# Edges read as 80 short rows and a written order for the first stage in a graph layer kernel

## The chip, the cores and the metric

The kernel runs on one core of a Trainium2 chip. The metric is the device time of one execution in microseconds (us), taken as the median of several runs. All profiles are of one execution on that core.

## What is computed

The reference is one layer of a graph transformer over 625 nodes of width 1024 with 20,000 edges. The first norm feeds a two-layer graph convolution and a linear attention, whose outputs are added to x; then a mixture of eight experts is added. Cut to what matters here:

```
xn = layernorm(x)
deg = segment_sum(ones, dst);  deg_inv = 1 / max(deg, 1)
sage(h, Ws, Wn, b) = h @ Ws + (segment_sum(h[src], dst) * deg_inv) @ Wn + b
gnn = sage(relu(sage(xn, Ws0, Wn0, b0)), Ws1, Wn1, b1)
q, k, v = xn @ Wq, xn @ Wk, xn @ Wv
mix = softmax(q over features) * 1/8 @ (softmax(k over nodes)^T @ v) @ Wo + bo
x = x + gnn + mix
x = x + moe(layernorm(x))
```

The edges come sorted by dst. The sum over edges is done as a product with a 625 x 625 matrix of edge counts, which the kernel counts from src and dst.

## The kernel before, in words

All float32 products are made of three matmuls on rounded parts. A tensor is split into a high part (a cast on ScalarE) and a low part (a subtraction on VectorE or GpSimd); `split` at L96 does both, so every such pair has line L96. `xnh` and `xnl` are the two parts of the transposed first norm, `whi` and `wlo` those of a weight tile. A weight tile is 512 KB, is loaded by SyncE's queue into `wraw` (three buffers, L121) and is split when `Stream.next` (L127) hands it out. Its argument says which engine does the low part; without one it is VectorE.

**The first stage.** The 625 rows of x are five tiles of 128 rows (the last has 113). SyncE's queue issues tiles 0 and 1, the edge lists, one key weight tile, then tiles 2 to 4 (L305 to L311). The edge lists `src` and `dst` are read as 10 rows of 2000 numbers each into `ei` (L308). Each x tile gets its statistics (`first_stats`, L250 and L251), its scale (`inv_std`, L254 to L260, a chain of tiny VectorE operations with one square root on ScalarE), is normalised in place (`first_norm`, even tiles on VectorE L330, odd ones on ScalarE L328) and is transposed on TensorE and split into `xnh` and `xnl` (`first_turn` to `to_t`, L278 and L96). Tiles 0 and 1 share one scale chain, tiles 2 to 4 another.

**The edges.** `edges` is the float copy of `ei` (L336), over 10 partitions. 32 small transposes (L340) and one more for the first dst of each row (L345) put 125 edges on 125 partitions: a chunk is 125 edges, a group is 16 chunks, and there are 10 groups, 160 chunks in all. GpSimd derives `field`, `srow` and `unit` (L438 to L446) and makes `edst` relative to the first dst of its group.

**The counting.** For each chunk VectorE writes a pair of one-hot matrices, 125 x 128 each (`one_hot`, L456 and L457), into a ring `hot` of 40 places. TensorE multiplies each pair (L479) and sums the 16 chunks of a group in `pa`; VectorE adds that to `packed` at a column that it reads from a register (L481, L483). A pair is written only when its place in the ring has been multiplied.

**The key steps.** `keys_step` makes K and the self product of the first convolution: 16 weight tiles, four steps each, 64 steps. A step is 12 matmuls (L400 to L402). The first three weight tiles take the columns of x tiles 0 and 1 first (256 columns, steps 0 to 5), then the other 370 columns (steps 6 to 11); the rest take 314 and 312. After a key tile is complete `keys_exp` takes its maximum over nodes on VectorE (L378), negates it (L379) and exponentiates on ScalarE (L380); a few steps later `keys_back` transposes it on TensorE into `pskt` (L372). In the main loop (L499 to L502) each step is followed by four one-hot pairs and the product of four chunks; 36 pairs are made ahead of it (L495).

**What sets the order.** Each engine has one queue, in strict order. A scheduler places instructions by priority; `tc.high_priority()` raises a block, `keep` (keep_in_program_order) fixes the order of the marked instructions on their engine, and `issue_after` holds something behind a named instruction. Before, only the loads, the statistics' first operation, some transposes and GpSimd's edge chain are marked.

## Time and profile before

| what | us |
|---|---|
| median of three runs | 1042.17 |
| lowest, highest run | 1039.62, 1044.56 |
| the profiled execution | 1041.26 |
| its span | 1039.7 |
| TensorE busy in it | 1010.3 |
| VectorE, ScalarE, GpSimd busy | 601.3, 396.2, 175.6 |
| first key matmul starts | 25.13 |
| one-hots written | 36.61 to about 129 |
| chunk products | 56.2 to 143.8 |

PE is TensorE's matmul, PEld its weight load, DVE VectorE, ACT ScalarE, POOL GpSimd and SP SyncE. A line of the page's second part has 40 digits, each the busy share in tenths of one fortieth of the span, here 26 us. A line of the timeline has the start, the length, the engine, the line of code, the operation, the tiles written and read, their sizes, and in brackets how long the engine had been idle and what ended that. A line of the waits names who waited for whom, the total, how often, and the longest. The times come from one profiled execution, and the text compares its sum with that execution's own time.

### The profile page before, as it was taken

The numbers are of one execution on the slowest core, as the hardware profiler recorded it, in microseconds if no ns is written. First come the engines' busy times: TensorE is split into PE (matmuls) and PEld (weight loads), VectorE is DVE, ScalarE is ACT, GpSimd is POOL, SyncE is SP. The second block draws the span as 40 slices with busy tenths as digits, with TensorE's granted clock in tenths as the row PEclk, the third lists the DMA queues.
The fourth block names the chain that finished last, engine by engine and source line by source line (L and its number), as shares of the span: only waits on it lengthen the run. The fifth ranks groups of instructions, "written<-read, shape, count | busy, mean of one in ns | idle before, by whom it ended". The sixth has DMA issues, their size and how long they took to land. (4 is left out here: it accounts for less than half of the span.)

```text
span 1039.7 us, 14793 instructions
## 1 busy us (share of the span) xinstructions
PE 1010.3 (97%) x5571; PEld 871.6 (84%) x5571; DVE 601.3 (58%) x1192; ACT 396.2 (38%) x577; POOL 175.6 (17%) x222
## 2 busy tenths in 40 slices
PE   6889999999999999999999999999999989999998
PEld 4889998888888887988877899998879777887786
DVE  3899941653253233733327536358687688887681
ACT  3333432232231122222114332246556567766610
POOL 2421001121035300200000103022121033120030
PEclk7999999999999999999999999999999999999999
DMA  6122225665234421232220125666967798897971
GB/s 186 56 67 59 64 77 187 234 205 198 79 111 151 160 82 64 67 115 78 82 81 21 42 63 189 191 184 189 284 235 229 243 304 293 288 290 247 329 260 51
DMA packets 111312, 164.68 MB, mean 158 GB/s; under 512 B 5919, under 2 KB 63271, under 8 KB 111230
## 3 DMA queue, kind: packets, MB, share of 16 engines
q1 hardware_dynamic: 97774, 118.54, 35.9%
q0 software_dynamic: 13456, 45.08, 12.9%
q8 instruction: 47, 0.77, 0.3%
q14 instruction: 35, 0.29, 0.1%
HBM read 133.19 MB, written 30.42 MB: 157 GB/s over the span
## 5 line engine op out<-in xcount | busy, mean ns | idle before, releaser
L96 DVE TENSOR_TENSOR wlo<-wraw,whi 128x1024 fp32r<-128x1024 f32 x140 | 178.1, 1272 | 263.1 <-ACT whi L96 262.0
L96 ACT CAST whi<-wraw 128x1024 fp32r<-128x1024 f32 x149 | 156.4, 1051 | 290.0 <-PE psg L207 66.2
L1137 PE MATMUL pse<-xs,whi 128*128 128x448 f32 (+1 forms) x384 | 109.1, 357 | 0.0
L96 DVE TENSOR_TENSOR wlo<-wmore,whi 128x1024 fp32r<-128x1024 f32 x67 | 87.0, 1299 | 26.8 <-ACT whi L96 25.7
L1133 PE MATMUL pse<-xs,wlo 128*128 128x224 f32 (+1 forms) x384 | 89.7, 254 | 0.1
L96 ACT CAST whi<-wmore 128x1024 fp32r<-128x1024 f32 x67 | 70.5, 1052 | 47.7 <-PE psz L207 18.5
L400 PE MATMUL psk<-xnh,whi 128*128 128x314 f32 (+3 forms) x256 | 82.9, 325 | 0.4 <-ACT xnh L96 0.4
L401 PE MATMUL psk<-xnl,whi 128*128 128x314 f32 (+3 forms) x256 | 79.6, 311 | 0.9 <-DVE xnl L96 0.8
L402 PE MATMUL psk<-xnh,wlo 128*128 128x314 f32 (+3 forms) x256 | 79.5, 311 | 0.2 <-POOL wlo L96 0.2
L1189 PE MATMUL psy<-wlo,he 128*128 128x512 f32 (+1 forms) x176 | 70.0, 398 | 3.3 <-DVE wlo L96 3.0
L1133 PEld LDWEIGHTS pse<-xs,wlo 128*128 128x128 f32 x384 | 72.0, 190 | 1.4 <-DVE wlo L96 0.3
L1137 PEld LDWEIGHTS pse<-xs,whi 128*128 128x128 f32 x384 | 69.0, 189 | 2.4
L1188 PE MATMUL psy<-whi,he 128*128 128x512 f32 (+1 forms) x176 | 69.4, 394 | 0.0
L1190 PE MATMUL psy<-whi,he 128*128 128x512 f32 (+1 forms) x176 | 69.0, 392 | 0.0
L457 DVE TENSOR_SCALAR hot<-iota,srow,unit 125x128 f16<-125x128 f16 x160 | 59.7, 373 | 0.0
L96 POOL TENSOR_TENSOR xs<-raw,xs 128x512 fp32r<-128x512 f32 (+2 forms) x24 | 34.4, 1454 | 115.6 <-ACT xs L96 95.0
L401 PEld LDWEIGHTS psk<-xnl,whi 128*128 128x128 f32 x256 | 49.5, 193 | 1.3 <-DVE xnl L96 1.3
L400 PEld LDWEIGHTS psk<-xnh,whi 128*128 128x128 f32 x256 | 49.2, 193 | 0.8 <-ACT xnh L96 0.8
L402 PEld LDWEIGHTS psk<-xnh,wlo 128*128 128x128 f32 x256 | 49.1, 192 | 0.4 <-POOL wlo L96 0.4
L456 DVE TENSOR_SCALAR hot<-iota,edt 125x128 f16<-125x128 f16 x160 | 45.8, 286 | 1.7 <-POOL edt L446 1.7
L1189 PEld LDWEIGHTS psy<-wlo,he 128*128 128x128 f32 (+1 forms) x176 | 31.8, 180 | 14.9 <-DVE wlo L96 6.7
L1188 PEld LDWEIGHTS psy<-whi,he 128*128 128x128 f32 (+1 forms) x176 | 31.9, 181 | 10.1
(348 smaller groups left out, 2379.5 us busy)
## 6 DMA issues: line engine op xcount, KB each, us to landing
wraw<-in_L_ffn_w_dram SPq DMA_DIRECT2D x65, 512.0 KB, 4.8
wmore<-in_L_ffn_w_dram SPq DMA_DIRECT2D x63, 512.0 KB, 5.4
xsd<-zt POOLq DMA_DIRECT2D x9, 1024.0 KB, 5.6
wraw<-in_L_gnn_W_self_dram SPq DMA_DIRECT2D x16, 512.0 KB, 3.7
wraw<-in_L_gnn_W_neigh_dram SPq DMA_DIRECT2D x16, 512.0 KB, 3.7
wraw<-_ffn_shared_gate_up_dram SPq DMA_DIRECT2D x16, 512.0 KB, 3.9
wraw<-in_L_mix_Wk_dram SPq DMA_DIRECT2D x8, 512.0 KB, 4.1
wraw<-in_L_mix_Wq_dram SPq DMA_DIRECT2D x8, 512.0 KB, 3.7
```

The costliest lines, as they stand in the source:

```text
L96: return (nc.scalar.copy(hi, srcap), (eng or nc.vector).tensor_sub(lo, srcap, hi.bitcast(F32)))
L400: nc.tensor.matmul(ps[:, :n], wh[:, kt, :], xnh[:, kt, c], start=kt == 0, stop=False)
L401: nc.tensor.matmul(ps[:, :n], wh[:, kt, :], xnl[:, kt, c], start=False, stop=False)
L402: nc.tensor.matmul(ps[:, :n], wl[:, kt, :], xnh[:, kt, c], start=False, stop=kt == KT - 1)
L456: nc.vector.tensor_scalar(h[:ET, :WIN], iota[:ET, :WIN], edst[:, i, g:g + 1], None, op0=ALU.is_equal)
L457: nc.vector.tensor_scalar(h[:ET, WIN:], iota[:ET, :WIN], srow[:ET, i, g:g + 1], unit[:ET, i, g:g + 1].bitcast(F32), op0=ALU.is_equal, op1= ...
L1133: nc.tensor.matmul(ps[a][:, :n], wl[:, k, c], xs[:, kt, 0, :], start=False, stop=False)
L1137: nc.tensor.matmul(ps[a][:, :2 * n], wh[:, k, c], xs[:, kt], start=kt == 0, stop=kt == KT - 1)
L1188: nc.tensor.matmul(acc, h(kt, 0), wh[:, k, :], start=kt == 0, stop=False)
L1189: nc.tensor.matmul(acc, h(kt, 0), wl[:, k, :], start=False, stop=False)
L1190: nc.tensor.matmul(acc, h(kt, 1), wh[:, k, :], start=False, stop=kt == KT - 1)
```

## The change

It has five parts.

1. The edge lists are read as 80 rows of 250 numbers (`EP` = 80), issued on ScalarE's queue, into small tiles of their own. Four transposes of 80 x 125 replace the 32, and `edt`, `field`, `srow` and `unit` get a new layout, [half, group, row in group]; which edges form a chunk changes within a group, not what a group holds. The big buffers no longer hold `ei` and `edges`.
2. SyncE's queue issues a key weight tile ahead of each of x tiles 2, 3 and 4.
3. Each x tile has a scale chain of its own (`first_scale`), and all are normalised on ScalarE.
4. The whole first stage is written out in one order, and nearly all its VectorE, ScalarE and GpSimd instructions are kept in it: two key steps, turn of tile 2, two steps, turn of tile 3, two steps, turn of tile 4. The edge transposes stand behind the turns of tiles 0 and 1.
5. In the counting, 40 pairs are made ahead; then three a step up to step 40 and four after it, made behind the products and no longer ahead of them. The register read for `packed` is held behind the last pair made so far. Key weight tiles 3 to 8 get their low part on VectorE, no longer on GpSimd.

The core of the diff:

```diff
+EP = E // (2 * ET)
...
-    ei = big.tile([128, 2, CH * ET], I32, name="ei", tag="big")
+    ei = edgep.tile([EP, 2, 2 * ET], I32, name="ei")
...
-    for t in range(2):
-        load_x(t)
+    load_x(0)
+    load_x(1)
     for i, e in enumerate((src, dst)):
-        keep(nc.sync.dma_start(ei[:NG, i, :], e.rearrange("(p c) -> p c", p=NG)))
-    st.load(1)
+        keep(nc.scalar.dma_start(ei[:, i, :], e.rearrange("(p c) -> p c", p=EP)))
     for t in range(2, NT):
+        st.load(t - 1)
         load_x(t)
...
+    def first_scale(t):
+        inv_std(lnv[:T, t:t + 1, 1], *(lnt[:T, i, t:t + 1] for i in range(3)), order=keep)
+        keep(nc.vector.scalar_tensor_tensor(lnt[:T, 1, t:t + 1], lnv[:T, t:t + 1, 0], -1.0, lnt[:T, 0, t:t + 1],
+                                            op0=ALU.mult, op1=ALU.mult))
+
+    def first_norm(t):
+        p = rows(t)
+        keep(nc.scalar.activation(xts[p, t, :], xts[p, t, :], AF.Identity,
+                                  bias=lnt[p, 1, t:t + 1], scale=lnt[p, 0, t:t + 1]))
...
+    def turn_edges():
+        pse = bank("psed")[:, :4 * EP].rearrange("p (a b) -> p a b", b=EP)
+        for i in range(4):
+            nc.tensor.transpose(pse[:ET, i, :], edges[:, i // 2, (i % 2) * ET:(i % 2 + 1) * ET], ident[:EP, :EP])
+        keep(nc.scalar.copy(edt[:ET].rearrange("p a h g j -> p (a h) (g j)"), pse[:ET]))
...
-        if s in (0, 2, 4):
-            wks[o] = st.next(nc.gpsimd)
         if (o, i, h) == (1, 1, 0):
-            wks[3] = st.next(nc.gpsimd)
+            wks[3] = st.next()
         if i == 0 and h == 0 and 2 < o < 2 * KT - 1:
-            wks[o + 1] = st.next(nc.gpsimd if o < KT else None)
+            wks[o + 1] = st.next()
...
+    def keys_weights(o):
+        wks[o] = st.next(nc.gpsimd, order=keep)
...
     with tc.high_priority():
-        keys_steps(4)
+        first_stats(0)
+        first_scale(0)
+        first_norm(0)
+        keep(nc.scalar.copy(edges, ei))
+        first_stats(1)
+        first_scale(1)
+        keys_weights(0)
+        first_norm(1)
+        first_stats(2)
+        first_turn(0)
+        first_turn(1)
+        turn_edges()
+        keys_weights(1)
+        first_scale(2)
+        first_norm(2)
         first_stats(3)
+        first_scale(3)
+        keys_weights(2)
+        first_norm(3)
+        keys_steps(2)
+        first_turn(2)
         first_stats(4)
-        first_norm(2, NT)
-        first_turn(2, keep)
+        first_scale(4)
+        first_norm(4)
         keys_steps(2)
-        first_turn(3, keep)
-        last = first_turn(4, keep)
+        first_turn(3)
+        keys_steps(2)
+        last = first_turn(4)
...
+                with tc.issue_after(hots[-1].ins):
+                    first_v = nc.vector.value_load(first_col[0:1, g:g + 1], min_val=0, max_val=N - 1)
...
-        one_hots(RING - 4)
+        one_hots(RING)
...
     while ks[0] < 8 * KT:
         keys_steps(1)
-        one_hots(4)
         count_chunks(4)
+        one_hots(3 if ks[0] < 5 * KT else 4)
```

The gathers of 128 rows are the indirect reads of the experts' outputs near the end; the change leaves them as they are.

More of the change, by code (lines that the diff above doesn't have):

```diff
@@ L93, in bank, with split @@
         return psum.tile([128, 512], F32, name=name, tag="ps")
-    def split(srcap, hi, lo, eng=None):
-        return (nc.scalar.copy(hi, srcap), (eng or nc.vector).tensor_sub(lo, srcap, hi.bitcast(F32)))
+    def split(srcap, hi, lo, eng=None, order=lambda ins: ins):
+        return (order(nc.scalar.copy(hi, srcap)), order((eng or nc.vector).tensor_sub(lo, srcap, hi.bitcast(F32))))
     class Stream:
@@ L125, in load, with next @@
                 self.loaded += 1
-        def next(self, eng=None):
+        def next(self, eng=None, **order):
             if self.ready:
@@ L139, in next @@
                 lo = wts.tile([128, D], F32R, name="wlo", tag="wlo")
-            split(r, hi, lo, eng)
+            split(r, hi, lo, eng, **order)
             b = ap.shape[2]
@@ L250, in stats, with inv_std @@
                 order(nc.vector.bn_stats(st6[:mv.shape[0], h, :], xt[:, h * 512:(h + 1) * 512]))
-        nc.vector.bn_aggr(mv, st6[:mv.shape[0]])
-    def inv_std(var, y, z, a):
-        nc.vector.tensor_scalar(a, var, EPS, None, op0=ALU.add)
-        nc.scalar.activation(y, a, AF.Sqrt)
-        nc.vector.reciprocal(y, y)
-        nc.vector.tensor_mul(z, y, y)
-        nc.vector.tensor_mul(z, z, a)
-        nc.vector.tensor_scalar(z, z, -0.5, 1.5, op0=ALU.mult, op1=ALU.add)
-        nc.vector.tensor_mul(y, y, z)
+        (order or (lambda ins: ins))(nc.vector.bn_aggr(mv, st6[:mv.shape[0]]))
+    def inv_std(var, y, z, a, order=lambda ins: ins):
+        order(nc.vector.tensor_scalar(a, var, EPS, None, op0=ALU.add))
+        order(nc.scalar.activation(y, a, AF.Sqrt))
+        order(nc.vector.reciprocal(y, y))
+        order(nc.vector.tensor_mul(z, y, y))
+        order(nc.vector.tensor_mul(z, z, a))
+        order(nc.vector.tensor_scalar(z, z, -0.5, 1.5, op0=ALU.mult, op1=ALU.add))
+        order(nc.vector.tensor_mul(y, y, z))
     def normalise(eng, yt, xt, mean, y, z):
@@ L271, in by_k, with to_t @@
         return nat.rearrange("p (c k) -> p k c", k=KT)
-    def to_t(nat, t, hi, lo, order=None):
+    def to_t(nat, t, hi, lo, order=None, both={}):
         for g in range(2):
@@ L280, in to_t @@
                     order(tr)
-            done = split(ps[:, :, rows(t)], hi[:, 4 * g:4 * g + 4, cols(t)], lo[:, 4 * g:4 * g + 4, cols(t)])
+            done = split(ps[:, :, rows(t)], hi[:, 4 * g:4 * g + 4, cols(t)], lo[:, 4 * g:4 * g + 4, cols(t)],
+                         **both)
         return done
@@ L318, in first_stats @@
         stats(xts[rows(t), t, :], lnv[rows(t), t, :], order=keep)
-    def first_norm(a, b):
-        inv_std(lnv[:T, a:b, 1], lnt[:T, 0, a:b], lnt[:T, 1, a:b], lnt[:T, 2, a:b])
-        y, z = lnt[:T, 0, :], lnt[:T, 1, :]
-        nc.vector.scalar_tensor_tensor(z[:, a:b], lnv[:T, a:b, 0], -1.0, y[:, a:b], op0=ALU.mult, op1=ALU.mult)
-        for t in range(a, b):
-            p = rows(t)
-            xt = xts[p, t, :]
-            if t % 2:
-                nc.scalar.activation(xt, xt, AF.Identity, bias=z[p, t:t + 1], scale=y[p, t:t + 1])
-            else:
-                nc.vector.tensor_scalar(xt, xt, lnv[p, t, 0:1], y[p, t:t + 1], op0=ALU.subtract, op1=ALU.mult)
@@ L332, in first_turn @@
-    def first_turn(t, order=None):
-        return to_t(xts[rows(t), t, :].rearrange("p (k c) -> p k c", c=128), t, xnh, xnl, order)
-    edges = big.tile([128, 2, CH * ET], F32, name="edges", tag="big")
-    nc.scalar.copy(edges[:NG], ei[:NG])
-    edt = edgep.tile([128, 2 * CH, NG], F32, name="edt")
-    pse = bank("psed")[:, :2 * CH * NG].rearrange("p (a b) -> p a b", b=NG)
-    for i in range(2 * CH):
-        nc.tensor.transpose(pse[:ET, i, :], edges[:NG, i // CH, (i % CH) * ET:(i % CH + 1) * ET], ident[:NG, :NG])
@@ L341, in gps_layer @@
-    nc.scalar.copy(edt[:ET], pse[:ET])
-    esrc, edst = edt[:ET, :CH, :], edt[:ET, CH:, :]
-    psf = bank("psf")
-    nc.tensor.transpose(psf[:, :NG], edges[:NG, 1, 0:1].to_broadcast([NG, 128]), ident[:NG, :NG])
+    def first_scale(t):
+        inv_std(lnv[:T, t:t + 1, 1], *(lnt[:T, i, t:t + 1] for i in range(3)), order=keep)
+        keep(nc.vector.scalar_tensor_tensor(lnt[:T, 1, t:t + 1], lnv[:T, t:t + 1, 0], -1.0, lnt[:T, 0, t:t + 1],
+                                            op0=ALU.mult, op1=ALU.mult))
@@ new lines, in first_norm, with first_turn @@
+    def first_norm(t):
+        p = rows(t)
+        keep(nc.scalar.activation(xts[p, t, :], xts[p, t, :], AF.Identity,
+                                  bias=lnt[p, 1, t:t + 1], scale=lnt[p, 0, t:t + 1]))
+    def first_turn(t):
+        return to_t(xts[rows(t), t, :].rearrange("p (k c) -> p k c", c=128), t, xnh, xnl, keep, dict(order=keep))
+    edges = edgep.tile([EP, 2, 2 * ET], F32, name="edges")
+    edt = edgep.tile([128, 2, 2, NG, CH // 2], F32, name="edt")
+    esrc, edst = edt[:ET, 0], edt[:ET, 1]
@@ L346, in gps_layer @@
     first_dst = edgep.tile([128, NG], F32, name="first_dst")
-    nc.scalar.copy(first_dst, psf[:, :NG])
     first_col = edgep.tile([1, NG], I32, name="first_col")
-    with tc.high_priority():
-        for t in range(2):
-            first_stats(t)
-        first_norm(0, 2)
-        first_stats(2)
-        for t in range(2):
-            first_turn(t)
+    def turn_edges():
[3 more added lines that the diff above has]
+        keep(nc.scalar.copy(edt[:ET].rearrange("p a h g j -> p (a h) (g j)"), pse[:ET]))
+        psf = bank("psf")
+        nc.tensor.transpose(psf[:, :EP], edges[:, 1, 0:1].to_broadcast([EP, 128]), ident[:EP, :EP])
+        keep(nc.scalar.copy(first_dst, psf[:, :EP].rearrange("p (g j) -> p g j", g=NG)[:, :, 0]))
@@ L422, in keys_steps @@
                 keys_step(k)
+    def keys_weights(o):
+        wks[o] = st.next(nc.gpsimd, order=keep)
     with tc.high_priority():
-        keys_steps(4)
-        first_stats(3)
+        first_stats(0)
[13 more added lines that the diff above has]
+        first_norm(2)
+        first_stats(3)
+        first_scale(3)
[3 more added lines that the diff above has]
+        first_turn(2)
         first_stats(4)
-        first_norm(2, NT)
-        first_turn(2, keep)
+        first_scale(4)
+        first_norm(4)
         keys_steps(2)
-        first_turn(3, keep)
-        last = first_turn(4, keep)
-    field = edgep.tile([128, CH, NG], F32, name="field")
-    srow = edgep.tile([128, CH, NG], F32, name="srow")
-    unit = edgep.tile([128, CH, NG], I32, name="unit")
+        first_turn(3)
+        keys_steps(2)
+        last = first_turn(4)
+    field = edgep.tile([128, 2, NG, CH // 2], F32, name="field")
+    srow = edgep.tile([128, 2, NG, CH // 2], F32, name="srow")
+    unit = edgep.tile([128, 2, NG, CH // 2], I32, name="unit")
     keep(nc.gpsimd.tensor_scalar(field[:ET], esrc, 1.0 / T, -0.496, op0=ALU.mult, op1=ALU.add))
@@ L445, in gps_layer @@
                                  op0=ALU.mult, op1=ALU.add))
-    keep(nc.gpsimd.tensor_sub(edst, edst, first_dst[:ET, None, :].to_broadcast([ET, CH, NG])))
+    keep(nc.gpsimd.tensor_sub(edst, edst, first_dst[:ET, None, :, None].to_broadcast([ET, 2, NG, CH // 2])))
     keep(nc.gpsimd.tensor_copy(first_col, first_dst[:1]))
@@ L455, in one_hot @@
     def one_hot(h, i, g):
-        nc.vector.tensor_scalar(h[:ET, :WIN], iota[:ET, :WIN], edst[:, i, g:g + 1], None, op0=ALU.is_equal)
-        nc.vector.tensor_scalar(h[:ET, WIN:], iota[:ET, :WIN], srow[:ET, i, g:g + 1],
-                                unit[:ET, i, g:g + 1].bitcast(F32), op0=ALU.is_equal, op1=ALU.mult)
-    pa, made, counted = [None], [0], [0]
+        e = (slice(0, ET), i // 8, g, slice(i % 8, i % 8 + 1))
+        nc.vector.tensor_scalar(h[:ET, :WIN], iota[:ET, :WIN], edst[e], None, op0=ALU.is_equal)
+        return nc.vector.tensor_scalar(h[:ET, WIN:], iota[:ET, :WIN], srow[e], unit[e].bitcast(F32),
+                                       op0=ALU.is_equal, op1=ALU.mult)
+    pa, made, counted, hots = [None], [0], [0], []
     def one_hots(n):
@@ L466, in one_hots @@
                 made[0] += 1
-                one_hot(hot[:, c % RING, :], c % CH, c // CH)
+                hots.append(one_hot(hot[:, c % RING, :], c % CH, c // CH))
     def count_chunks(n):
@@ L480, in count_chunks @@
             if i == CH - 1:
-                first_v = nc.vector.value_load(first_col[0:1, g:g + 1], min_val=0, max_val=N - 1)
+                with tc.issue_after(hots[-1].ins):
+                    first_v = nc.vector.value_load(first_col[0:1, g:g + 1], min_val=0, max_val=N - 1)
                 to = packed[:T, ds(first_v, WIN)]
@@ L559, in recount @@
         ct = tmp.tile([128, HW], F32, name="ct", tag="tmp")
-        nc.vector.tensor_tensor(edst, edst, first_dst[:ET, None, :].to_broadcast([ET, CH, NG]), op=ALU.add)
+        nc.vector.tensor_tensor(edst, edst, first_dst[:ET, None, :, None].to_broadcast([ET, 2, NG, CH // 2]), op=ALU.add)
         nc.vector.tensor_scalar(field[:ET], esrc, float(HW), None, op0=ALU.is_ge)
@@ L569, in recount @@
                     h = tmp.tile([128, WIN + HW + 1], F16, name="hrare", tag="tmp")
-                    nc.vector.tensor_scalar(h[:ET, :WIN], iota[:ET, :WIN], edst[:, i, ds(g, 1)], None, op0=ALU.is_equal)
-                    nc.vector.tensor_scalar(h[:ET, WIN:WIN + HW], iota[:ET, :HW], esrc[:, i, ds(g, 1)],
-                                            field[:ET, i, ds(g, 1)], op0=ALU.is_equal, op1=ALU.mult)
+                    nc.vector.tensor_scalar(h[:ET, :WIN], iota[:ET, :WIN], edst[:, i // 8, ds(g, 1), i % 8], None, op0=ALU.is_equal)
+                    nc.vector.tensor_scalar(h[:ET, WIN:WIN + HW], iota[:ET, :HW], esrc[:, i // 8, ds(g, 1), i % 8],
+                                            field[:ET, i // 8, ds(g, 1), i % 8], op0=ALU.is_equal, op1=ALU.mult)
                     nc.tensor.matmul(ps[:, :HW], h[:ET, :WIN], h[:ET, WIN:WIN + HW], start=i == 0, stop=i == CH - 1)
```

## The prediction

> **What bounds the kernel now.** I read the page first, then the waits of TensorE, then the timeline of the first 75 us engine by engine.

> From the page: busy time, the slices and the clock.

> ```profile
> span 1039.7 us, 14793 instructions
> PE 1010.3 (97%) x5571; PEld 871.6 (84%) x5571; DVE 601.3 (58%) x1192; ACT 396.2 (38%) x577; POOL 175.6 (17%) x222
> ...
> PE   6889999999999999999999999999999989999998
> ...
> PEclk7999999999999999999999999999999999999999
> ```

> TensorE bounds nearly everything; its low slices are the first three. The waits of PE (total us, times, longest) name its idle time:

> ```profile
> PE psed L340 <- ACT edges L336: 6.8, 1, 6.8
> PE pskt L372 <- ACT shared L380: 3.0, 1, 3.0
> PE psy L1189 <- DVE wlo L96: 3.0, 4, 1.5
> PE pst L278 <- DVE xts L330: 2.0, 1, 2.0
> ```

> No PE wait from 175 us on ends with a weight transfer, so a PE that starts earlier should end earlier. The timeline (start, length) gives the stage that the change rewrites:

> ```profile
> 11.09 3.51 ACT L336 CAST edges<-ei 10x4000 f32<-10x4000 int32 x1
> ...
> 14.74 6.86 PE L340 MATMUL psed<-ident,edges 10*125 10x10 f32 x32 [6.75 <-ACT edges L336]
> ...
> 42.05 0.43 PE L401 MATMUL psk<-xnl,whi 128*128 128x370 f32 x1 [0.80 <-DVE xnl L96]
> 65.64 0.77 PE L372 MATMUL pskt<-ident,shared 128*128 128x128 f32 x5 [2.96 <-ACT shared L380]
> ```

> A cast over ten rows, then 32 tiny transposes, stand in PE's queue ahead of the first x transposes, normalised since 11.2. From 42.05 PE streams 370 columns every 0.17 us; it stops once more, 62.68 to 65.64. That stop begins on VectorE, which reaches the maximum for the exp late, having lost time three times like this (DVE, then POOL):

> ```profile
> 47.23 2.50 DVE L457 TENSOR_SCALAR hot<-iota,srow,unit 125x128 f16<-125x128 f16 x1
> 47.27 2.40 POOL L96 TENSOR_TENSOR wlo<-wraw,whi 128x1024 fp32r<-128x1024 f32 x1 [10.57 <-ACT whi L96]
> ```

> A one-hot of 0.31 us lasts as long as POOL's instruction beside it; again at 54.42 (2.41), 56.75 (2.43) and, later, at 67.01, 79.71 and 87.22. The stop is paid twice (windows: span, busy PE, PEld, DVE, ACT, POOL, clock):

> ```profile
> 67.00:68.00 1.00, 1.00 (x6) 1.00 (x6) 1.00 (x2) 0.16 (x1) 1.00 (x1) 0.54 0.00 0
> 68.00:69.00 1.00, 1.00 (x7) 0.81 (x6) 1.00 (x1) 0.00 (x0) 1.00 (x1) 0.50 0.00 0
> ```

> Matmuls stand 0.26 apart instead of 0.145 from 67.1 to 70.4: 3.3 us at half rate, 1.6 lost.

> **Part 1: the first stage, up to key step 6 (PE at 42.05).** PE's order after that point is unchanged, so I carry the new queues forward to it, with before's durations.

> Arrivals: x0 is used at 4.53. Ahead of x2 now stand x0, x1 and Wk0; x2 was used at 11.18 and has the 20 edge rows of 8 KB no longer before it on its queue, so I take 10.9 at latest. The 7 us slice moved 73 GB/s where its neighbours move 295 and 166: that was the edge rows. Now they are 160 rows of 1000 bytes, issued on ACT after its table load: two issues of 0.41 and 0.30 (their SP rows) from 2.5, where ACT idles. They should land by 8; no row shows it, so from 5 (x0 landed 3.6 after its issue) to 12 (the slowest landing of the stage, 10 after issue). Up to 9 is free; each us later is a us in ACT's queue (sqrt 1, whi 0, norm 1 stand behind the cast).

> Scale and norm: statistics and aggregate 1.53 (4.53 to 6.06); from there to the scaled mean 1.62. DVE: tile 0 ready 7.7, tile 1 10.9. The norms of tiles 0, 2 and 4 move from DVE (0.81) to ACT (1.24), which I count there. ACT: norm 0 (1.24) to 8.95, cast of 500 elements a row (3.51 x 500/4000, with overhead 0.5) to 9.5, sqrt 1, whi 0 (1.05) to 10.75, norm 1 to 12.15. PE: turn 0 at 9.0, turn 1 at 12.2.

> [...] Before, the clock fell to half at 12.5, after PE idled from 8.0, and rose at 26.1, 4.5 us after the x transposes began at 21.6. [...] 12.5, 26.1, 67.1, 70.4 lie whole multiples of 3.41 apart; a window 42% busy fell, one 60% busy did not. [...] with half clock from 12.5 to 15.9 turn 1 lasts to 14.0, the five edge transposes (0.2 each) to 15.1. By before's row of half clock to 26.1, stage 1 would lose 4 more. [...]

> Then: xnh (0.59 each) to 14.6; edge copies 0.43 and 0.17 to 15.6; whi 1 to 16.65. Steps 0-1, 24 matmuls of 0.12, from 15.1, partly at half clock, to 18.4. POOL's wlo 1 runs 16.7 to 19.05 and the scale of tile 2 meets it: before, L254 took 2.21 instead of 0.17 beside such an instruction. So scale 2 ends at 19.5 (18.1 without that). Norm 2 to 20.75, turn 2 20.8 to 21.9, steps 2-3 to 24.8 (wlo 1 in time). ACT: psk copy 0.37, sqrt 3, whi 2 to 22.5, xnh, norm 3 to 24.3, xnh to 24.85; wlo 2 at 24.95. Turn 3 to 25.9, steps 4-5 to 28.8. DVE: two xnl to 25.55, statistics 4 to 27.05, scale 4 to about 29 beside POOL's small operations; norm 4 to 30.2, turn 4 from there, xnh at 31.3, xnl at 31.95. PE is at the point of 42.05 at 31.95: **10.1 sooner**. ACT carries about 18 of those 24 us and sets the pace; PE waits 1.4 for norm 4. Bounds: 12 if no lock or half clock bites, 6 if half clock stays to 26 and some ten handovers cost 0.2 more. Nearest to the rows used: 10.

> **Part 2: the keys and the counting.** Removed: six POOL splits (2.4 each), each stopping a one-hot for some 2.15: 13 us. What POOL then does before its fill at 162 is nothing, so no one is let through earlier there. Added: the same splits on DVE, 1.27 each (the row of L96 DVE): 7.6. Queued behind each on DVE are the one-hots; waiting for it are PE's next key tile and, in the new order, the negated maximum. 40 pairs are made ahead instead of 36, then 3 a step.

> From the issue order of the changed program: 11.5 pairs, wlo 3, max 0, 28.5 pairs, max 1, wlo 4, mx 1. A pair costs 0.385 (twelve from 42.45 to 47.06). Pairs start at 32.55; POOL's field chain, 4.9 from 24.95, is done at 30. wlo 3 ends at 38.35 (its whi waits for step 7, 36.0), max 0 at 39.1, exp 0 with its table load 41.6; PE asks at 44.15, so no wait. 28 pairs to 50.3, max 51.0, wlo 4 52.25, exp 1 53.35. PE asks 20.63 after step 6 as before (62.68 - 42.05), at 52.6: a wait of **0.8** replaces 2.96, too short for the clock. The transposes of 65.64 come at 53.4, 12.2 sooner, and the 1.6 of half clock goes: **13.8**.

> After that a group of four steps takes PE 8.75 and DVE 12 x 0.385 + 0.72 + 1.27 + 0.15 + 0.29 = 7.05: PE stays the bound, cover 1.7. At four pairs a step it is 16 x 0.385 + 1.6 = 7.8, still under. Counting ends at the same step; register loads stand directly ahead of an add now too (90.40, no gap), so nothing. The DMA issues moved ahead on SP are of the same count; x4 now waits for x0 to land (4.5), needed at 25: nothing. The edge tiles leave the six big buffers, and the same six are then held by the same tiles: nothing. Bounds of part 2 beyond part 1: 1.5 (DVE two us later: 2.8 waited, half clock again) to 4.5 (no wait).

> **Sum.** Profiled execution 1041.3 (span 1039.7) - 13.8 = 1027.5. It lies 0.9 under the median 1042.2, so 1028.

> **Rivals.**
> Half clock stays and ACT's handovers pile up: gain 6 + 2 to 4, say 9, so **1033**. For: ACT is one chain of some 30 instructions, each waiting on another engine. Against: PE's sustained work starts at 12.2 rather than 21.6.
> Cleaner start: no lock, windows fall well: 12 + 4.5, **1025**.
> No gain: the weight stream is the true pace from 800 us on, where DMA is 0.89 busy, and takes the gain back: **1042**. For: that share. Against: no PE wait there names a transfer.
> Slower: DVE becomes the bound of the counting. If splits between the pairs break their overlap, a pair costs its two page means, 286 + 373 ns = 0.66. By 0.275 a pair: 28 pairs delay exp 1 by 7.7; six groups cost 12 x 0.275 - 1.7 = 1.6 each, 9.6; the last two and a half, 16 x 0.275 - 1 = 3.4 each, 8.5. 25.8 - 13.8 = 12 slower, **1054**. It decides from a pair of about 0.57. Against: 0.385 is the spacing wherever POOL is still.
> That the change does not do what it says is ruled out by the issue order.

> **Chances.** Likeliest 0.68 (own range 1024 to 1032), half clock 0.18, cleaner 0.06, no gain 0.05, slower 0.03. The range 1022 to 1035 takes the first three with the spread of the runs (1039.6 to 1044.6). A change under 0.5% can't be told from none here; faster by more means under 1037: 0.92, same 0.05, slower 0.03.

> **What would show it.** Right: the first key matmul at 14 to 16 (25.13 before), the 370-column stream at 30 to 34, the second pskt at 52 to 56 with a wait under 1.4, clock 1.0 there, no one-hot over 0.5 us until 140. Wrong: edges landing after 12; half clock beyond 19; DVE waits on the new splits; PE waits on pa or wlo after 60; or a wait on wraw late in the kernel.

## The result and the profile after

The changed kernel took 1031.96 us (median of 4 runs, 1029.49 to 1032.83) beside 1042.51 for the kernel before on the same chip (4 runs). The ratio is 0.9897, with a 95% interval of 0.9867 to 0.9927. Run once more, unchanged, it took 1029.82 (6 runs) beside 1039.9, a ratio of 0.9891 (0.9867 to 0.9915). So it is about 1% faster, and the gain is 10 to 11 us where 13.8 was forecast. The profiled execution of the changed kernel took 1032.83 with a span of 1031.2, 8.5 under the span before.

The page after (the head, busy times, TensorE's slices and its clock):

```profile
span 1031.2 us, 14763 instructions
PE 1004.8 (97%) x5543; PEld 866.2 (84%) x5543; DVE 595.3 (58%) x1216; ACT 397.7 (39%) x583; POOL 160.2 (16%) x216
...
PE   7999999999999999999999999999999999999798
...
PEclk8999999999999999999999999999999999999899
```

The first slices are better, as intended. But at the right end, slice 38 of both lines, there is a new dip of TensorE and of its clock, which the kernel before does not have there. The count has changed too: 28 matmuls fewer (5571 before), and as many weight loads. Both facts turn out to be the same story.

TensorE's waits after name the new idle time:

```profile
PE pst L279 <- ACT xts L329: 5.8, 4, 1.9
PE psz L206 <- issue: 5.2, 1, 5.2
```

The wait of 6.8 for the cast of the edges is gone, and the 3.0 before the second `pskt` is down to 0.6. Four handovers from ScalarE in the first stage cost 5.8. The second line is new in size: 5.2 us in which nothing that the profile records holds TensorE back. It is just behind a branch.

The early part went nearly as worked out (timeline of the changed kernel: start, length, and in brackets idle time and releaser). These are the cast of the edges, their transposes, the matmul that answers to 42.05 before, and the second `pskt`, at 65.64 before:

```profile
9.12 0.59 ACT L424 CAST edges<-ei 80x500 f32<-80x500 int32 x1
14.06 0.97 PE L345 MATMUL psed<-ident,edges 80*125 80x80 f32 x4
31.87 0.44 PE L393 MATMUL psk<-xnl,whi 128*128 128x370 f32 x1
53.05 0.77 PE L366 MATMUL pskt<-ident,shared 128*128 128x128 f32 x5 [0.56 <-ACT shared L374]
```

The last chunk is multiplied at 129.7 (143.8 before) and the last matmul of the experts' second product, `psy`, starts 14.2 sooner, at 964.6 where it was 978.8. Then come a branch at L1255 (L1237 before) around a loop for experts with more rows than their places, which is jumped over here, and the last product of all, the shared expert's `psz`. Here is that place in the kernel before, from the timeline:

```profile
978.80 0.39 PE L1190 MATMUL psy<-whi,he 128*128 128x512 f32 x1
980.63 0.47 PE L205 MATMUL psz<-whi,sth 128*128 128x512 f32 x1 [1.45 <-DVEq L1237]
```

And in the changed kernel:

```profile
964.57 0.39 PE L1208 MATMUL psy<-whi,he 128*128 128x512 f32 x1
970.12 0.77 PE L206 MATMUL psz<-whi,sth 128*128 128x512 f32 x1 [5.16 <-issue]
```

The wait rose from 1.45 to 5.16. The windows behind it (length, then busy time and count of PE, PEld, DVE, ACT, POOL; then the clock, the share of the DMA engines, GB/s) show a second price:

```profile
968.00:969.00 1.00, 0.00 (x0) 0.00 (x0) 0.00 (x0) 0.00 (x0) 0.00 (x0) 0.50 0.72 223
971.00:972.00 1.00, 1.00 (x4) 0.71 (x4) 0.00 (x0) 0.00 (x0) 0.54 (x1) 0.50 1.01 377
```

The clock was at half from 967.8 to 974.6. In that stretch the matmuls stand 0.43 us apart, behind it 0.23. The count in brackets takes in every matmul that reaches into the window, so it is no count of starts. From the first `psz` to the end it takes 61.08 (1031.2 - 970.12), before 59.07 (1039.7 - 980.63). So 3.7 of wait and 2.0 of slower matmuls give back 5.7 of the 14.2, and 8.5 is left, which is the difference of the spans.

```profile
q8 instruction: 1, 0.02, 6.0%
```

```profile
q8 instruction: 1, 0.02, 6.3%
```

By its times in the trace, the packet before ran from 973.65 to 974.61, so it began about 5.5 ahead of the end of the products at 979.2; none ran in the wait itself. After, there is none from 960 on until one that ran from 967.62 to 968.63, 2.7 us into the wait that began at 964.96; the first `psz` follows its end by 1.5. The edges lost 28 transposes with their weight loads, 56 TensorE instructions, so everything behind them moved up by 56 places in the stream. The place at which the next block is fetched, if it is tied to the count, did not move. 28 matmuls at the 0.227 of their spacing here are 6.4 us: by this estimate the fetch that came about 5.5 ahead of the jump should come about 1 behind it; it is seen 2.7 behind it. By the code the jump is over some 230 instructions. At which count a packet is asked for, no run here shows. The rival was that the transfers around that jump, which keep the DMA engines busy (share 0.72 and 1.01 in the two windows above), happened to hold something up in this run.

### The profile page after: what moved, and what is told of

Its sections match the earlier page's. It is cut to its first block, busy times and chain, and to the rows that moved or that the text cites. A ratio compares the mean times of both kernels' runs of the same rounds, so it can differ in the third digit from the quotient of the medians.

```text
span 1031.2 us, 14763 instructions
## 1 busy us (share of the span) xinstructions
PE 1004.8 (97%) x5543; PEld 866.2 (84%) x5543; DVE 595.3 (58%) x1216; ACT 397.7 (39%) x583; POOL 160.2 (16%) x216
## 5 line engine op out<-in xcount | busy, mean ns | idle before, releaser
L97 DVE TENSOR_TENSOR wlo<-wraw,whi 128x1024 fp32r<-128x1024 f32 x146 | 185.0, 1267 | 266.3 <-ACT whi L97 262.0
L97 ACT CAST whi<-wmore 128x1024 fp32r<-128x1024 f32 x67 | 70.4, 1051 | 53.4 <-PE psz L208 24.3
L474 DVE TENSOR_SCALAR hot<-iota,srow,unit 125x128 f16<-125x128 f16 x160 | 49.8, 311 | 0.0
L1206 PEld LDWEIGHTS psy<-whi,he 128*128 128x128 f32 (+1 forms) x176 | 31.9, 181 | 10.1
L473 DVE TENSOR_SCALAR hot<-iota,edt 125x128 f16<-125x128 f16 x160 | 40.1, 251 | 0.2 <-issue 0.2
```

What stands on the lines that cost most here:

```text
L97: return (order(nc.scalar.copy(hi, srcap)), order((eng or nc.vector).tensor_sub(lo, srcap, hi.bitcast(F32))))
L473: nc.vector.tensor_scalar(h[:ET, :WIN], iota[:ET, :WIN], edst[e], None, op0=ALU.is_equal)
L474: return nc.vector.tensor_scalar(h[:ET, WIN:], iota[:ET, :WIN], srow[e], unit[e].bitcast(F32), op0=ALU.is_equal, op1=ALU.mult)
L1206: nc.tensor.matmul(acc, h(kt, 0), wh[:, k, :], start=kt == 0, stop=False)
```

## The experiments

Twelve kernels were run, in four groups. Each group shares the runs of the kernel before, whose median was 1039.9 in the first (16 runs), 1040.4 in the second (30), 1042.0 in the third (10) and 1040.8 in the fourth (11). "Key step 6" is here the matmul that answers to 42.05 of before, and "last chunk" the last chunk's product, at 143.8 before.

### The wait at the jump

**Unchanged** (again):

> The changed kernel once more, nothing edited. Theory A (the loss at the end is a fetch of a 16 KB block of TensorE's instructions, set by how many instructions stand before the jump over the overflow experts): the wait ahead of the first psz is again 5 to 5.3 us and the time again 10 to 11 us under the kernel before. Theory B (the fetch met other traffic in that one execution): the wait is 1 to 3 us this time, and the profiled time some 4 us lower.

1029.82. The wait was 4.06, again put down to `issue`, with half clock behind it. That is less than the 5 to 5.3 of theory A and more than the 1 to 3 of theory B. Key step 6 came at 31.08 and the last chunk at 128.9. A chance in one run it is not.

**More warm-up matmuls** (page28):

```diff
-WARM = 20
+WARM = 48
-        nc.tensor.matmul(psw, cold[:, :128], cold, start=i == 0, stop=i == WARM - 1)
+        nc.tensor.matmul(psw[:, :213], cold[:, :128], cold[:, :213], start=i == 0, stop=i == WARM - 1)
```

> The changed kernel with its 20 warm-up matmuls of 512 columns cut into 48 of 213: the same array time, and 28 pairs of weight load and matmul more, which is what the edge transposes lost, so that every later TensorE instruction has the place it had before the change. Theory A: the wait ahead of the first psz is 1.4 us as before the change, no half clock after it, and the time is 5 to 6 us under the unedited changed kernel, about 1026. Theory B: the wait is what it was, and the time within 1.5 us of the unedited changed kernel.

1026.15 (ratio 0.9853, 0.9828 to 0.9877), 3.7 under the unchanged one, where 5 to 6 was expected. The wait is 1.45 and no half clock follows. The gain on the kernel before is now 13.75. In its profile key step 6 was later, at 33.03: of its two windows of half clock in the first stage one fell on 22.4 to 25.8, where in the unchanged run both lie together, 13.6 to 20.4. But the warm-up is different too, so by itself this run did not prove the case.

**Fewer of them** (pagem8), `WARM = 12`, 16 instructions less than the changed kernel:

> The changed kernel with 12 warm-up matmuls instead of 20, so 16 TensorE instructions fewer. [...] Theory A: no fetch ahead of the first psz (1 to 2 us), but the next block is asked for late too, so up to 3 us may be lost some 30 instructions on; time 2 to 6 us under the unedited changed kernel, less what a colder clock in the first 10 us costs (under 1.5). Theory B: the same 5 us wait or a random one.

1029.4 (0.9892, 0.9866 to 0.9917), the changed kernel's own time; the profile is of the slowest of its six runs, 1034.91. The wait did not vanish and did not stay; it moved (timeline):

```profile
969.79 0.47 PE L206 MATMUL psz<-whi,sth 128*128 128x512 f32 x1 [1.45 <-DVEq L1255]
970.10 0.40 PE L207 MATMUL psz<-wlo,sth 128*128 128x512 f32 x1
973.05 0.80 PE L208 MATMUL psz<-whi,stl 128*128 128x512 f32 x1 [2.55 <-issue]
```

TensorE passes the jump, does a few matmuls and then stands, in the middle of a run of products, and the view names no releaser. The packet of the fetch ran from 970.85 to 971.84, inside this stop.

**Instructions that never run** (unexecuted). 28 further matmuls are put inside an earlier branch, the one for rare edges at L776, whose body is jumped over:

```diff
-                    nc.tensor.matmul(ps[:, :n], g0h[rows(s), s, o * 128:(o + 1) * 128], al[rows(s), c0:c0 + n],
-                                     start=True, stop=True)
+                    for _ in range(29 if (s, o, c0) == (0, 0, 0) else 1):
+                        nc.tensor.matmul(ps[:, :n], g0h[rows(s), s, o * 128:(o + 1) * 128], al[rows(s), c0:c0 + n],
+                                         start=True, stop=True)
```

> The changed kernel with 28 further matmuls and weight loads inside the branch for rare edges, whose body is jumped over and never executed: everything that runs is the changed kernel's, in its order, and only the place of TensorE's later instructions in its stream moves, by 56, to where it was in the kernel before. If the place of the branch over the overflow experts decides: the wait there is 1.45 to 2.2 instead of 4.1 to 5.2 and no half clock follows, and the time falls by 3 to 5 from 1029.8, to 1025 to 1027, with the first stage as it was (key step 6 at 30 to 31). Rival: the version with 28 more warm-up pairs gained its 3.7 in the first stage, by other warm-up matmuls; then the wait or the time stays, at 1029 to 1031.

1024.55 (1023.25 to 1026.47; ratio 0.984, 0.9815 to 0.9864), 5.3 under the changed kernel by code that nothing executes. The wait (timeline):

```profile
964.32 0.47 PE L206 MATMUL psz<-whi,sth 128*128 128x512 f32 x1 [1.49 <-DVEq L1256]
```

The page has 47 packets of q8 again, and the packet of the fetch is ahead again, as this line of the DMA view of 956 to 957 shows:

```profile
q8 instruction: 1, 0.02, 8.8%
```

From the first `psz` to the end it took 59.08 (1023.4 - 964.32), as before. The wait is 2.57 shorter than in the unchanged run and the rest 2.69 (61.77 there): together 5.3, the difference of the medians. TensorE came to the jump at 962.8 in both profiles. The rival of this run, that the first stage made the gain, falls: key step 6 was even later, at 33.14. (A window of half clock at 187.6 to 191.1 in the unchanged run, which this one lacks, made most of that up.)

**The kernel before, moved** (beforemoved): the same edit in the kernel before, with 100 matmuls (`range(101 ...)`). This number, like the 16 instructions of pagem8, comes from my estimate of where a block begins; no run here shows that place itself.

> The kernel before with 100 further matmuls and weight loads inside the same branch, never executed: 200 instructions[...]. If the place decides: the wait before the first psz rises from 1.45 to 4 or 5 and half clock follows it, and the time rises by 3 to 5.7, to 1043 to 1046 beside 1040.4. Rival: what matters is something else of the changed kernel (its transfers, the time at which it arrives); then the wait stays 1.45 and the time 1040 to 1041. The longer jump over the enlarged body may itself cost up to 2 by its wait before the first psag, which was 1.5.

1050.9 (1047.14 to 1052.1; ratio 1.0086, 1.0063 to 1.011), 10 slower, more than expected. Two waits of TensorE did it (the waits view; 1.4 and 1.5 in the kernel before):

```profile
PE psz L205 <- PEq L1238: 4.6, 1, 4.6
PE psag L785 <- DVE wlo L96: 4.0, 1, 4.0
```

The first is the one that was meant: 3.2 longer, with half clock from 986.3 to 993.1, and 61.45 from the first `psz` on instead of 59.07, in all 5.6. The second is the jump over the body that I had enlarged by 200 instructions. It waits 2.5 longer, with half clock from 412.8 to 419.6; I had allowed 2 for it. The releaser that the view names there is not what it waited for: a packet of the fetch ran from 410.69 to 412.11 in that wait, and the matmuls start at 413.51. So the place in the stream is shown to be the cause from both sides, in both kernels, without touching anything that runs.

**The fetch in all profiles.** That the link is the fetch is read from the packets of all fourteen profiles. In seven (before, page28, unexecuted, edgespage, oldedges, pagescale, scalefour) TensorE waits 1.45 to 2.16 at the jump, and the packet begins 5.0 to 6.4 us before TensorE gets there. In six (the profile after, again, beforemoved, edgesonly, lowpool, oldcount) it waits 3.23 to 5.16, and the packet begins 0.5 to 2.7 us after TensorE got there. In pagem8 the packet is in the later stop. In all these long stops, with the second one of beforemoved eight, the next matmul starts 1.2 to 1.8 us after the packet's end.

### Which part gives the 14

**The edges alone** (edgesonly): the kernel before with 80 rows on ScalarE's queue, four transposes and the new layout.

```diff
-        keep(nc.sync.dma_start(ei[:NG, i, :], e.rearrange("(p c) -> p c", p=NG)))
+        keep(nc.scalar.dma_start(ei[:, i, :], e.rearrange("(p c) -> p c", p=EP)))
...
-    for i in range(2 * CH):
-        nc.tensor.transpose(pse[:ET, i, :], edges[:NG, i // CH, (i % CH) * ET:(i % CH + 1) * ET], ident[:NG, :NG])
+    for i in range(4):
+        nc.tensor.transpose(pse[:ET, i, :], edges[:, i // 2, (i % 2) * ET:(i % 2 + 1) * ET], ident[:EP, :EP])
```

> The kernel before with the edges part alone: 80 rows on ACT's queue, four transposes, the tiles by halves. TensorE's instruction count is that of the changed kernel. If the edges are the main part of the early gain: key step 6 about 6 to 8 sooner than before (34 to 36 instead of 42.05), the stop before the second pskt about 3 as before, since GpSimd's low parts stay, the last product of the counting some 6 to 8 sooner; and by the instruction-block theory a wait of 4 to 5 at the jump and a half clock after it, which gives some 5.7 of that back: 1038 to 1040 in all. Rival: the written order, not the edges, makes the early gain; then key step 6 is at 40 or later and the time is 1042 or more, above before by the block's loss. Rival of the block theory: the wait at the jump stays 1.45, and the time is 1033 to 1035.

1039.03, ratio 0.9985 (0.9968 to 1.0002): no difference that can be told, over 20 runs from 1033.0 to 1044.6. Yet in its profile key step 6 is at 34.83 (7.2 sooner) and the last chunk at 134.4 (9.4 sooner). The wait at the jump is 4.1 and the end takes 60.4. So the largest part of the change, made alone, gives almost nothing. The profiled run is one of the shortest of the 20, 1033.84, so it does not show all of why.

**The edges alone, put back in place** (edgespage), with the 28 warm-up pairs of page28:

> The edges alone, as in the run of 1039.0, with the 28 further warm-up pairs that put the branch back to where it stood in the kernel before. If the block of instructions takes the edges' gain at the end: the wait at the jump is 1.45 to 2.2 instead of 4.1, no half clock follows it, the tail from the first psz on is near 59 instead of 60.4, and the median falls by 4 to 5.5, to 1033.5 to 1035. Rival: the wide spread of that run (1033.0 to 1044.6) is the loss by the clock in the first stage, and the block matters little there: 1037 or more.

1032.51, ratio 0.9918 (0.989 to 0.9946). The wait is 1.5. What the 28 pairs bring here is 0.7% of the time, about 7 us, more than the 2.6 of wait and 1.4 of the end that the two profiles differ by. The clock that each run lists holds the rest. Span times (1 - granted clock) is on average 12.3 us in the 20 runs of the edges alone and 6.4 in these 5, and what is left of the span is nearly equal, 1025.3 and 1025.2 (the clock is listed to 0.001, so to 1 us). A part of it is the half clock behind the jump. The other part would be where the windows of the clock fall and what the changed warm-up does to them; the runs do not separate these, and why the edges alone lose so much more to the clock stays open.

**The old edges in the new order** (oldedges): the changed kernel with ten rows of 8000 bytes, issued on ScalarE's queue, the cast over ten rows and 33 transposes.

```diff
-EP = E // (2 * ET)
+EP = NG
...
-        for i in range(4):
-            nc.tensor.transpose(pse[:ET, i, :], edges[:, i // 2, (i % 2) * ET:(i % 2 + 1) * ET], ident[:EP, :EP])
+        for i in range(2 * CH):
+            nc.tensor.transpose(pse[:ET, i, :], edges[:NG, i // CH, (i % CH) * ET:(i % CH + 1) * ET], ident[:NG, :NG])
```

> The changed kernel with the old edge tiles alone put back: ten rows of 8000 bytes (issued on ACT's queue), the cast over ten rows, 32 and one transposes, which here stand behind the first two x transposes. TensorE's instruction count is that of before. If the edges make most of the early gain: the cast of 3.5 stands in ACT's chain ahead of norm 1, the 32 transposes take 3 to 7 us of TensorE, key step 6 is at 36 to 39 (31.0 in the changed kernel), the last product of the counting 5 to 8 later than there, and, with a wait of 1.45 at the jump and no half clock after it, the whole is about 1030 to 1033, near the changed kernel. Rival: the order alone makes it, the edges are hidden behind it: step 6 at 31 to 33 and the whole at 1024 to 1026.

1035.35 (0.9945, 0.992 to 0.9971). It was slower than I expected: key step 6 at 41.80, only 0.25 sooner than before. The timeline shows the two lumps in the new queues:

```profile
10.07 3.51 ACT L424 CAST edges<-ei 10x4000 f32<-10x4000 int32 x1
...
18.06 6.89 PE L345 MATMUL psed<-ident,edges 10*125 10x10 f32 x32
```

The cast stands in ScalarE's chain ahead of the scale of tile 1, and the transposes run at half clock (11.9 to 29.0) ahead of all key steps. So the written order has nothing to give while the edges are in its way. The counting then gains: the last chunk is at 139.6, 4.2 sooner. By the last chunk, edges alone 9.4 and the rest alone 4.2 make 13.6, against 14.1 for all of it: the parts add up.

**The low parts of key tiles 3 to 8 back on GpSimd** (lowpool):

> The changed kernel with the low parts of key weight tiles 3 to 8 back on GpSimd. Theory A2 (part 2 of the prediction): one-hots beside them take 2.4 us again, the second pskt waits about 3 us and not 0.6, half clock follows for one window, so 3 to 5 us slower than the unedited changed kernel. Rival (the written order alone took that wait away): within 1 us of it.

1036.18 (0.9957, 0.9938 to 0.9976), 6.4 slower than the unchanged one, somewhat above the 3 to 5 expected. One-hots last 2.4 to 2.6 again beside GpSimd, the maximum is late, and TensorE stops for 3.98 (timeline):

```profile
43.34 2.55 DVE L474 TENSOR_SCALAR hot<-iota,srow,unit 125x128 f16<-125x128 f16 x1
43.45 4.75 POOL L97 TENSOR_TENSOR wlo<-wraw,whi 128x1024 fp32r<-128x1024 f32 x2 [3.77 <-ACT whi L97]
...
56.64 1.33 PE L366 MATMUL pskt<-ident,shared 128*128 128x128 f32 x5 [3.98 <-ACT shared L374]
```

In this stop the clock fell; it was at half from 55.7 to 62.5. The last chunk came at 136.0 instead of 128.9.

**The old counting** (oldcount): 36 pairs ahead, four pairs a step ahead of the products, no order on the register read; the splits stay on VectorE.

```diff
-        one_hots(RING)
+        one_hots(RING - 4)
...
         keys_steps(1)
+        one_hots(4)
         count_chunks(4)
-        one_hots(3 if ks[0] < 5 * KT else 4)
```

> The changed kernel with the old counting: 36 pairs ahead instead of 40, then four pairs behind each step's products without the order after the read of a register; the splits stay on VectorE. My working took the pairs in the order of the change and the splits' move together. If the removal of GpSimd's splits is all of it, the second pskt stays at 52 to 53 with a wait under 1, the last product of the counting is within 0.5 of the changed kernel's and the time within 1 of its 1029.8. Rival: the order matters by itself; then TensorE waits on one-hots or VectorE is late with a maximum or a low part, the counting ends 1 to 4 later and the time is 1031 to 1034.

1034.18 (0.9939, 0.9916 to 0.9962), 4.4 slower, so the order matters by itself, as the rival had it, but not where either theory looked. The second `pskt` does not wait at all (57.83). The loss is in the first stage (timeline):

```profile
28.60 0.46 POOL L462 TENSOR_TENSOR edt<-edt,first_dst 125x160 f32<-125x160 f32 x1
29.09 0.26 DVE L473 TENSOR_SCALAR hot<-iota,edt 125x128 f16<-125x128 f16 x1 [2.53 <-POOL edt L462]
29.26 0.20 DVE L252 BATCH_NORM_AGGREGATE lnv<-bnst 113x2 f32<-113x12 f32 x1
```

Only the 36 pairs made ahead are held behind the first stage. The ring has 40 places, so the four pairs of the first loop step have nothing to wait for, and the scheduler puts them into the scale chain of tile 4. There the first one waits for GpSimd's edge chain, and the aggregate of tile 4, done at 26.0 in the unchanged run, stands behind it until 29.26. Tile 4 is normalised 3.7 later, TensorE waits 3.9 for it, its clock is at half from 32.5 to 39.3, and the last chunk is 5.5 later (134.4). The kernel before had the same four pairs there, at 36.61 to 39.4. The three pieces of the counting's order (the pairs ahead, three or four a step, the register read) were not run apart.

### Can it be made better

**Scale 2 ahead of the second low part** (pagescale): page28 with

```diff
-        keys_weights(1)
         first_scale(2)
+        keys_weights(1)
         first_norm(2)
```

> The version with 28 further warm-up pairs, which gave 1026.2, and besides the scale of tile 2 issued ahead of the split of Wk tile 1, so that the multiply of 2.14 us no longer stands beside GpSimd's low part. If that lock sets when tile 2 is normalised, norm 2 starts near 17.5 instead of 19.8 and TensorE reaches key step 6 about 1 us sooner (less than 2, since steps 0 and 1 then keep TensorE busy to about 19.8 and the low part of Wk tile 1 comes later, near 22): 1025.2 against 1026.2. Rival: the low part, now later, meets the scale of tile 3 in the same way, and the time stays 1026.2 or loses up to 1. The wait at the jump over the overflow experts is 1.45 in both theories, since TensorE's instruction count is that of the 1026.2 version.

1023.75 (0.9831, 0.9803 to 0.9858). The median is lower than either theory gave, but by the intervals it can't be told from page28's 0.9853 (0.9828 to 0.9877). The "lock" of these texts is a VectorE operation that lasts as long as the GpSimd one beside it, here 2.40 beside 2.39. It moved, as the rival said (timeline):

```profile
19.97 2.39 POOL L97 TENSOR_TENSOR wlo<-wraw,whi 128x1024 fp32r<-128x1024 f32 x1 [0.62 <-ACT whi L97]
19.98 2.40 DVE L324 SCALAR_TENSOR_TENSOR lnt<-lnv,lnt 128x1 f32<-128x1 f32 x1
```

Norm 2 starts at 17.13 instead of 19.76, but norm 3 at 22.42 instead of 22.91, and key step 6 at 31.29. Against page28's profile that is 1.7 sooner: the gap ahead of tile 2's turn went from 2.77 to 0.28, and the window of half clock at 22.4 to 25.8 is gone. So what moved is the clock, in these two profiles.

**No scale beside GpSimd at all** (scalefour): Wk tile 2's low part on VectorE behind the scale of tile 4.

```diff
-        wks[o] = st.next(nc.gpsimd, order=keep)
+        wks[o] = st.next(nc.gpsimd if o < 2 else None, order=keep)
...
-        keys_weights(2)
         first_norm(3)
+        first_stats(4)
+        first_scale(4)
+        keys_weights(2)
         keys_steps(2)
         first_turn(2)
-        first_stats(4)
-        first_scale(4)
         first_norm(4)
```

> The version of 1023.75 with the low part of Wk tile 2 on VectorE, behind the scale of tile 4, and that tile's statistics ahead of the low parts of the x transposes of tile 2: so no scale stands beside a low part of GpSimd (in the 1023.75 version the last operation of the scale of tile 3 lasted 2.40 beside one). If the lock is what holds the last norms: norm 3 near 20.6 instead of 22.4, norm 4 near 25 instead of 28, key step 6 near 28.5 instead of 30.4, the time 1021.5 to 1022.5. Rival: TensorE now waits for the low part of Wk tile 2 (step 4 wants it near 23.2, it is done near 24.4) and for x4, which lands near 20, and the time stays at 1023 to 1025. The wait at the jump is 1.4 to 2.2 by both.

1022.97 (0.9815, 0.9788 to 0.9842), which can't be told from 1023.75. Norm 4 starts at 25.25, as expected, but norm 3 at 22.22 (20.6 expected), and key step 6 stays at 31.20: TensorE ran at half clock from 14.1 to 20.9 in this profile, and step 4 waited 0.9 for its low part. No wait for tile 4 is left, so by this profile TensorE's own work was the bound. The rival fits better. These two have the lowest medians, 1.7 and 1.85% under the kernel before and by the ratios 6 to 8 us under the changed one, but their intervals overlap those of unexecuted (0.984) and page28 too; most of the gain is the place of the branch.

## Why the prediction was nearly right, and where it failed

**Part 1, "10.1 sooner".** The matmul of 42.05 came at 31.87, 10.2 sooner. To be off by only 0.1 was luck: with the same first stage it came at 31.08 in the second profile and at 33.14 in unexecuted. The main lines hold: edges cast at 9.12 without waiting, turn 0 at 9.35, first key matmul at 14.8 (14 to 16 was given), norm 2 at 19.79, turn 3 at 24.88. Three details inside the sum were otherwise. I put GpSimd's lock on the first operation of scale 2. It fell on the first multiply of that chain (timeline):

```profile
16.58 2.38 POOL L97 TENSOR_TENSOR wlo<-wraw,whi 128x1024 fp32r<-128x1024 f32 x1 [3.39 <-ACT whi L97]
16.84 2.14 DVE L258 TENSOR_TENSOR lnt<-lnt 128x1 f32<-128x1 f32 x1
```

It took 2.14 instead of 0.16, about the length that I had taken from L254. Norm 4 started at 28.5, not 29. And half clock lasted to 18.9, two windows, not to 15.9, one; in the second profile to 20.4, past the 19 that was named as a sign of being wrong. A window here is the 3.41 us of which the stretches of half clock are made: up to the last 2 us of the span they last 13.65 and three times 3.41 in the profile of before, 6.83, 3.41, 3.41 and 6.83 in that of the changed kernel. That the first stage would have one was my estimate, from the one behind the 2.96 of wait in the profile of before (67.1 to 70.5), and I took it over the row of before, which lasted to 26.1. The runs lie between, one window in page28's first cold stretch, two in both profiles of the changed kernel and in scalefour's. The row of before had in fact spoken against one: from 15.9 to 22.7 TensorE was busy without a gap, mostly with the tiny edge transposes, for two windows (6.83 of 6.83 us), and the clock stayed at half. In oldedges, with the same transposes, it stayed there from 11.9 to 29.0. So a full row alone did not bring the clock back; what does stays open.

**Part 2, 13.8 in all.** The second `pskt` came at 53.05 after a wait of 0.56 (53.4 and 0.8 forecast), the clock stayed up there, no one-hot lasted over 0.33, and no wait of TensorE in the counting names a one-hot. Lowpool confirms that the splits' move carries this. What I priced at nothing, "40 pairs are made ahead instead of 36, then 3 a step", was worth about 4.4 (oldcount): it takes four pairs out of the scale chain of tile 4. The sum did not show the omission, because I carried the queues of the changed program forward, where these pairs are gone; but I did not see why they are.

At 965 us TensorE was 14.2 ahead (16.4 in the second profile), against 13.8. That was the mechanism, and it was right; the closeness again owes something to chance.

**The step that failed** is the first sentence after the waits: "No PE wait from 175 us on ends with a weight transfer, so a PE that starts earlier should end earlier." The shift was carried to the end as if nothing there depended on the instructions removed. The 28 transposes were priced by their time alone, and their place in the instruction stream was not looked at. The wait of 1.45 behind the branch was in the profile of before, too short to draw the eye. The runs put in its place 3.7 of wait and 2.0 of half clock (2.6 and 2.7 in the second profile). Put back in place without touching a running instruction, the changed kernel gains 16.2 on the kernel before (1040.8 - 1024.55), and with 28 warm-up pairs 13.75.

**The rivals.** The measured 1031.96 is only just inside the own range of 1024 to 1032, and nearer to the 1033 of "half clock stays" than to 1028. But that rival had the loss in the first stage, 6 gained there instead of 10, and 10.2 was gained; its number was near by chance. "No gain" guessed that the end would take the gain back, but by the weight stream. Part of it, 5.7 of 14.2, was taken back there, with a fetch of instructions. DVE as the bound, and half clock to 26, did not happen.

## What to carry to other kernels

Here 14.2 us saved ahead of a jump left 8.5 behind it, because the jump was met in another state: look at every wait behind a taken branch, and recount when instructions are added or removed ahead of it. When a part of a change looks worthless alone, look first for a wait put down to `issue` and for the clock behind it; a few instructions in a body that is never executed test that cheaply. Small operations that have no reason to wait can be placed early by a scheduler, as the four pairs of oldcount were, for 4.4 us: hold back all of them that depend on a slow chain, not only most.

## What the hardware showed that was not expected

- **Where an instruction lies.** Moving TensorE's stream by 56 instructions changed the wait behind one taken branch between 1.45 to 1.5 and 4.1 to 5.2 us; by 72 from there (pagem8 beside page28) it moved 2.55 of the wait a few matmuls past the jump. At the short waits a packet of the fetch began 5.0 to 6.4 us before TensorE got to the jump, at the long ones 0.5 to 2.7 after. That a jump over only some 230 TensorE instructions can have a wait of 5.16 behind it was new to me. In the enlarged body of beforemoved a jump longer by 200 instructions cost 2.5.
- **A stall costs twice.** Stops of 2.16 us and more at the jump or just behind it were followed by half clock in all eight profiles that have one, for 3.4 us (edgesonly, oldcount, pagem8, pagescale) or 6.8 us (after, again, beforemoved, lowpool), with some 1.4 to 2.7 us on top where that was measured; the waits of 1.45 to 1.90 in the other six were not.
- **The spread between runs is for the most part the clock.** Of the kernel before, the 30 spans of the second group run from 1035.9 to 1045.0. Span times granted clock runs from 1025.5 to 1029.4 only. The edges alone spread most, 1031.3 to 1042.9, and one profile of such a kernel is not its median. Part of it is chance: each of the fourteen profiles has a wait of 1.9 us for the second norm, at some 550 to 575 us; in six of them 3.4 us of half clock follow it (before at 568.8, after at 554.8), in eight none (again, unexecuted).
- **The lock reaches the smallest operations.** A VectorE multiply of one number a row, and a scalar_tensor_tensor of the same size, took 2.14 and 2.40 beside a GpSimd subtraction of 2.38 and 2.39, where their like take 0.16. When one scale was moved out of its way, the next one met it.
